# Ends of a two-layer attention and adjacency kernel: first loads by columns, biases of three pairs by accumulating transfers, the bias product on column tiles, a new order

## The chip, the cores and the metric

The kernel runs on one core of a Trainium2 chip. A core has a matrix engine (TensorE, PE in the profile, with its weight loads shown as PEld), a vector engine (VectorE, DVE), a scalar engine (ScalarE, ACT), a general engine (GpSimd, POOL) and an engine that mainly issues transfers (SyncE, SP). Each runs its own instructions in order and waits on semaphores for the others. Transfers between the device's memory (DRAM) and the core's memory (SBUF) are issued by SP, ACT or POOL into queues and carried out by 16 DMA engines. Matrix products go into PSUM, which here is used as eight banks of 128 x 512 f32.

The metric is the device time of one execution in microseconds (us), the median over several runs. The profile is of one execution, which has its own time.

## The reference

Two layers on x of 64 x 256 x 512 (f32), with an adjacency matrix adj of 256 x 256 zeros and ones, 8 heads of 64:

```python
q = (x @ Wq + bq).reshape(b, n, H, HD)          # k, v alike
scores = jnp.einsum('bqhd,bkhd->bhqk', q, k) / jnp.sqrt(jnp.float32(HD))
scores = scores + (1.0 - adj)[None, None, :, :] * -1000000000.0
attn = jax.nn.softmax(scores, axis=-1)
out = jnp.einsum('bhqk,bkhd->bqhd', attn, v).reshape(b, n, d)
x = _layernorm(x + (out @ Wo + bo))             # layer 0
y = jnp.einsum('nm,bmd->bnd', adj, x)
x = _layernorm(x + (y @ W1 + b1))               # layer 1
```

The layer norm has no weights: it subtracts the mean over the 512 features and divides by the root of the variance plus 1e-5.

## The kernel before

**Tiling.** The 64 batches are taken as 32 pairs, p = 0 to 31. A pair has 512 rows, so a product of a pair with a 512 x 512 matrix is four *blocks*, `block(name, p, j)`, each of one bank (`product`, L311 to L337). Names are q, k, v (projections), o (times Wo) and l (times W1). q and k are made transposed, features on partitions; `j` counts feature tiles there and row tiles elsewhere. Heads come in two halves of four (g = 0, 1).

**Precision.** An f32 product is made of three products in the faster type fp32r. Each operand is split into a high part, a low part and a scaled difference (`x_high` and `x_rest` for x, `set_high` and `rest` for the others, `split_high`, `split_rest`, `split_scale` for weights), and a block is 3 x 4 matmuls of 128x512, in the order low, high, diff (`operands`). The high part is a copy on ACT, low and diff are two instructions on DVE, the scale of a weight's low part is again on ACT. Only the first half of pair 0's q and k are plain f32 products of unsplit weights (4 matmuls, each in two halves in the trace).

**Weights.** There is no room for all split weights. A ring of six 1 MB tiles `wr` holds two stages of three parts; `STAGES` (L100) lists them: qk1, v, qk0, then for each pair v, qk1, o, qk0 of the next, l of the last. The first time, a stage is split from raw weights in the ring (`ring_high`, `ring_rest`, `ring_scale`: L122, L127/L128, L131, four steps each) and kept in DRAM (`keep`, POOL). From then on `load_w` (L114, POOL) loads the three parts when `end_stage` has freed a stage. `steps_of` cuts the twelve steps of a stage into four lists, which `start`, `first` and `second` put between blocks.

**Attention.** `scores(p, g)` makes eight banks of logits in matmuls of 64 rows (L414) and the exponentials on ACT (L427); `masked` (L433) multiplies by the adjacency on DVE, two per batch, and `summed` (L441) adds the two key halves. `values(p, g)` multiplies the sums with ones (L370) and the exponentials with v (L380), both on 32-column tiles of the array, copies the banks out on ACT (zc L372, vc L384) and divides on DVE (L387 to L399). Between the two batches of values an argument `between` puts other work.

**Residuals and norms.** `load_r` brings a pair's x as residual R (1 MB, SP). `biased` (L450) adds bo or b1 to one batch of R, 128x1024 on DVE; a block of o or l is added to R while it is evicted (L324, DVE), with the row sums. Then `mean` (DVE), `squared` (ACT), `inverse` (DVE, then a power on POOL, L476), `less` (DVE) and `normed` (L487, ACT), which for l also issues the output. `hl_high` (ACT) and `hl_low` (DVE) split the result, and `adj_x` (L514) multiplies it by the adjacency.

**Start.** SP loads the four row tiles of pair 0's x, bq, bk, Wv, adj, pair 1's x in 128-byte runs (`load_x`, 4 transfers for each of 4 tiles), Wo, bv, bo, b1; ACT's queue loads halves of Wq and Wk (256 columns each). `x_first` (L237) transposes pair 0's x on TensorE against an identity made on POOL, 16 transposes, and copies each 128x128 out alternately on DVE and ACT. `square_adj` checks adj for numbers that aren't finite. `bv_wo` (L226) folds bv into bo, since bv times Wo is the same for all rows: bv is widened to 128 columns, four f32 matmuls make the product in all 128 rows, and DVE adds it to bo.

**Order.** Pairs are pipelined by hand: `first(w)` and `second(w)`, for w = 1 to 30, hold the second half of pair w - 1's attention, pair w's projections, o and l of pair w - 1 and the first q and k of pair w + 1. `start` comes before, `ending` behind. On PE, DVE and ACT instructions run in the order in which these functions write them (L640 to L649); POOL and SP are ordered by a scheduler. A check (`n_good`) at the end decides whether a general version must run instead; with these inputs it doesn't.

Of the kernel before, what the change touches and what calls it, by code (L numbers as in the profile page):

```python
# [8 lines left out]
F32 = mybir.dt.float32  # L9
F32R = mybir.dt.float32r  # L10
I32 = mybir.dt.int32
AF = mybir.ActivationFunctionType
# [23 lines left out]
def fast(tc, x, adj, wq, bq, wk, bk, wv, bv, wo, bo, w1, b1, out):  # L36
# [33 lines left out]
    RAW, SCRATCH, W, UNCUT = {}, {}, {}, {}  # L70
# [17 lines left out]
    def by_partition(b, name):  # L88
        t = cpool.tile([P, DC], F32, name=name)
        nc.sync.dma_start(t, b.rearrange("(c p) -> p c", p=P))  # L90
        return t
# [75 lines left out]
    rows0 = []  # L167
    for i in range(4):
        t = four.tile([P, D], F32, name="low")
        nc.sync.dma_start(t, xc[0, i // 2, i % 2])  # L170
        rows0.append(t)
    for which, w in (("q", wq), ("k", wk)):
        RAW[which] = two.tile([P, DC, D], F32, name="r")
        nc.scalar.dma_start(RAW[which][:, :, 0:HF], w.rearrange("(c p) e -> p c e", p=P)[:, :, 0:HF])
# [3 lines left out]
    bq_s, bk_s = by_partition(bq, "bq"), by_partition(bk, "bk")  # L178
# [3 lines left out]
    for which, w in (("q", wq), ("k", wk)):  # L182
        nc.scalar.dma_start(RAW[which][:, :, HF:], w.rearrange("(c p) e -> p c e", p=P)[:, :, HF:])
    adj_s = two.tile([P, NC, N], F32, name="vc")
    nc.sync.dma_start(adj_s, adj.rearrange("(c p) m -> p c m", p=P))
    for i in range(4):
        load_x(1, i)
    for k in range(DC):
        if k % 2 == 0:
            raw_o = two.tile([P, 2, D], F32, name="hl")  # L190
        RAW["o", k] = raw_o[:, k % 2]
        nc.sync.dma_start(RAW["o", k], wo[k // 2 * HF:(k // 2 + 1) * HF].rearrange("(h a i) e -> a h i e", h=4, a=2)[k % 2])
    bv_s = cpool.tile([P, DC], F32, name="bv")
    for d in range(DC):
        nc.sync.dma_start(bv_s[:, d:d + 1], bv.rearrange("(g h a i u) -> g a h i u", h=4, a=2, i=32, u=1)[d // 2, d % 2])
# [8 lines left out]
    power = cpool.tile([P, 2], F32, name="power")  # L204
    nc.gpsimd.memset(power, -0.5)
    adjT = cpool.tile([P, NC, N], F32R, name="adjT")
# [10 lines left out]
    def square_adj():  # L217

        square = two.tile([P, NC, N], F32, name="vc")
        nc.vector.tensor_tensor(square, adj_s, adj_s, op=OP.mult)  # L220
        nc.vector.tensor_tensor(square, square, adj_s, op=OP.not_equal)
        nc.vector.memset(acc, 0.0)
        nc.vector.tensor_reduce(acc[:, 0, 0:1], square, AX.XY, OP.max)
        nc.vector.tensor_scalar(acc, acc, RANGE * RANGE, None, op0=OP.mult)

    def bv_wo():  # L226

        wide = one.tile([P, DC, P], F32, name="z")
        nc.vector.tensor_copy(wide, bv_s[:, :, None].to_broadcast([P, DC, P]))
        pm = banks.tile([P, D], F32, name="ps")  # L230
        for d in range(DC):
            nc.tensor.matmul(pm, wide[:, d, :], RAW["o", d], start=d == 0, stop=d == DC - 1)
        nc.vector.tensor_tensor(bo_s, bo_s, pm, op=OP.add)
# [3 lines left out]
    def x_first(i):  # L237
        if i == 0:
            for d in range(DC):
                if d % 2 == 0:  # L240
                    t = one.tile([P, 2, D], F32, name=f"e{2 + d // 2}")
                XF[0, d] = t[:, d % 2]
# [3 lines left out]
        for d in range(DC):  # L246
            to = XF[0, d][:, i * P:(i + 1) * P]
            if d % 2:
                nc.scalar.activation(to, pt[:, d], AF.Copy)
            else:  # L250
                nc.vector.tensor_copy(to, pt[:, d])
# [41 lines left out]
    def operands(name, p, j, k):  # L293
# [15 lines left out]
        return [pairs[i] for i in (1, 0, 2)]  # L309

    def product(name, p, j):  # L311
        pm = banks.tile([P, D], F32, name="ps")
        pairs = [operands(name, p, j, k) for k in range(DC)]
        n = len(pairs[0])
        for i in range(n):
            for k in range(DC):
                nc.tensor.matmul(pm, *pairs[k][i], start=i == 0 and k == 0, stop=i == n - 1 and k == DC - 1)  # L317
# [130 lines left out]
    def biased(p, b, bias):  # L448
        if 0 <= p < NP:
            nc.vector.tensor_tensor(R[p][b], R[p][b], bias[:, None, :].to_broadcast([P, NC, D]), op=OP.add)  # L450
# [7 lines left out]
    def mean(p, name, b, cs=slice(0, 2)):  # L458
        if 0 <= p < NP:
            if cs.start == 0:  # L460
                ln = small.tile([P, 4, 2], F32, name="ln")
# [21 lines left out]
    def normed(p, name, j):  # L483
        if 0 <= p < NP:
            b, c = divmod(j, 2)
            t, r = LN[p, name, b], R[p][b][:, c]
            nc.scalar.activation(r, r, AF.Identity, scale=t[2][:, c:c + 1], bias=t[3][:, c:c + 1])  # L487
# [46 lines left out]
    def first(w, more=([], [], [], [])):  # L534

        q, n = w - 1, w + 1
        values(q, 1, ([(x_t, n, 0), (x_t, n, 1), (squared, q - 1, "l", 2)], [(squared, q - 1, "l", 3)]))
        scores(w, 0)
        do((inverse, q - 1, "l", 1), masks(w, 0, 0),
# [15 lines left out]
    def second(w, more=([], [], [], [])):  # L555
        q, n = w - 1, w + 1
        values(w, 0, ([(squared, q, "o", 2), (hl_low, q, 0, 0), (hl_low, q, 0, 1)], [(squared, q, "o", 3)]))
        scores(w, 1)
        masks1 = masks(w, 1, 1)
        do((inverse, q, "o", 1), (with_b1, q, 0), masks(w, 1, 0), more[0],  # L560
           (block, "q", n, 0), (less, q, "o", 1), (normed, q, "o", 2), (normed, q, "o", 3), masks1[:1],
           (adj_x, q, 0, 0), (hl_high, q, 1, 0), (hl_low, q, 1, 0), masks1[1:2], more[1],
           (block, "k", n, 0), (adj_x, q, 0, 1), (hl_high, q, 1, 1), (hl_low, q, 1, 1),
           (qk_high, "q", n, 0), (qk_rest, "q", n, 0), (qk_high, "k", n, 0), (qk_rest, "k", n, 0), more[2],
           (block, "q", n, 1), (adj_x, q, 1, 0), (k_low, n, 0), (qk_high, "q", n, 1), more[3], masks1[2:],
           (block, "k", n, 1), (stage_end, n), (adj_x, q, 1, 1), (qk_high, "k", n, 1), (qk_rest, "q", n, 1),
           (block, "l", q, 0), (qk_rest, "k", n, 1), (k_low, n, 1), (block, "l", q, 1), (with_b1, q, 1),
# [9 lines left out]
    def start():  # L577
        do(*((x_first, i) for i in range(4)), *((x_high, 0, i) for i in range(4)))
        qk1, v, qk0 = (steps_of(*stage) for stage in STAGES[:3])
        do((block, "q", 0, 0), (x_rest, 0, 0), (x_rest, 0, 1), qk1[0], (block, "k", 0, 0), (x_rest, 0, 2), (x_rest, 0, 3), qk1[1],  # L580
           (block, "q", 0, 1), qk1[2], v[0], (block, "k", 0, 1), (square_adj,), (adj_t,), qk1[3])
        scores(0, 0)
        do(v[1], masks(0, 0, 0), (block, "q", 0, 2), v[2], (qk_high, "q", 0, 2), (qk_rest, "q", 0, 2), (x_t, 1, 0), (x_t, 1, 1), v[3],
           (block, "k", 0, 2), (x_high, 1, 0), (x_high, 1, 1), (qk_high, "k", 0, 2), (qk_rest, "k", 0, 2), masks(0, 0, 1),
           (block, "q", 0, 3), (k_low, 0, 2), (qk_high, "q", 0, 3), (qk_rest, "q", 0, 3), (x_rest, 1, 0), (x_t, 1, 2),
           (block, "k", 0, 3), (stage_end, 0), (qk_high, "k", 0, 3), (qk_rest, "k", 0, 3), (x_rest, 1, 1), (x_t, 1, 3), qk0[0],
           (block, "v", 0, 0), (k_low, 0, 3), (x_high, 1, 2), (x_rest, 1, 2), (block, "v", 0, 1), qk0[1],
           (block, "v", 0, 2), (x_high, 1, 3), (x_rest, 1, 3), qk0[2], (block, "v", 0, 3), qk0[3], (stage_end, 0), (load_r, 0), (load_l,))
        values(0, 0)
        scores(0, 1)  # L590
        qk0 = [(f, name, 1, j) for j in range(2) for name in "qk" for f in (qk_high, qk_rest)]
        do((bv_wo,), (block, "q", 1, 0), masks(0, 1, 0), qk0[:2], (block, "k", 1, 0), qk0[2:4], masks(0, 1, 1),
           (block, "q", 1, 1), (k_low, 1, 0), qk0[4:6], (o_high, 0, 0, 0), (o_high, 0, 1, 0), (o_rest, 0, 0, 0),
           (block, "k", 1, 1), qk0[6:], (stage_end, 0), (k_low, 1, 1), (o_rest, 0, 1, 0))

    def ending():
# [37 lines left out]
           (inverse, p, "l", 0), (normed, q, "l", 3),  # L634
# [203 lines left out]
```

## Time and profile before

| what | value |
|---|---|
| time, three runs | 2412.70, 2413.47, 2413.59 us; median 2413.47 |
| the profiled execution's own time | 2412.73 us |
| its span (first to last recorded work) | 2411.0 us |
| DVE's commonest: masked, 128x1024 | 299.7 us in 252, mean 1221 ns |
| squares of the norms on ACT, 128x512 | 184.0 us in 256, mean 719 ns |
| normed on ACT, 128x512 | 194.9 us in 256 (some records hold two), mean of a record 809 ns |
| power on POOL | 152.6 us in 129, mean 1183 ns |
| loads of split weights, 1 MB each | median from issue to landing: 6.8 (v), 7.6 (qk), 8.2 (o), 8.3 (l) us |
| keeps of split weights, 1 MB each | median 9.6 us |
| moved by the DMA engines | 603.45 MB, mean 250 GB/s |

A timeline row is written "start, duration, engine, line, operation, output <- inputs, shape, count", and in brackets the idle time of the engine before it and what ended it. A line number is that of the kernel before. A product's record of 512 f32r columns is about 0.39 long, but matmuls overlap in the pipeline, and a new one starts about every 0.23. The 40 slices of the span show TensorE at 90% or more in all but the first (80 to 90%) and the last (70 to 80%).

### The profile page before, as it was taken

How to read it: one execution, taken by the hardware profiler on the slowest of the kernel's cores; microseconds unless marked ns; L12 is line 12 of the kernel's file. 1: busy time of each engine (PE TensorE's matmuls, PEld its weight loads, DVE VectorE, ACT ScalarE, POOL GpSimd, SP SyncE). 2: the span in 40 equal slices, each digit the busy share in tenths (PEclk: the TensorE clock that was granted, in tenths of full speed). 3: DMA queues.
4: the chain of work that ended last, by engine and by line, in shares of the span. 5: the costliest groups of instructions: out<-in, count | busy, mean ns of one | idle time of the engine just before them, and what ended most of it. 6: DMA issues, size and time to landing. Idle time of an engine off the chain costs nothing.

```text
span 2411.0 us, 42905 instructions
## 1 busy us (share of the span) xinstructions
PE 2382.0 (99%) x16894; PEld 1908.6 (79%) x16894; DVE 2003.9 (83%) x3320; ACT 1504.1 (62%) x2796; POOL 449.5 (19%) x736
## 2 busy tenths in 40 slices
PE   8999999999999999999999999999999999999997
PEld 5778878888778878788887788787888877888876
DVE  7898888888888988888888889888888888898876
ACT  5666665666666666656656566566566565665655
POOL 0111121121121211211212111112122121112111
PEclk9999999999999999999999999999999999999999
DMA  7777787777887777977778877779768788777661
GB/s 251 273 230 266 257 282 260 233 246 257 262 290 243 229 266 253 292 256 229 254 258 262 280 243 237 258 255 299 253 224 261 258 262 274 241 236 261 241 240 37
DMA packets 370719, 603.45 MB, mean 250 GB/s; under 512 B 272848, under 2 KB 275152, under 8 KB 310224
## 3 DMA queue, kind: packets, MB, share of 16 engines
q0 software_dynamic: 67824, 493.91, 55.5%
q1 hardware_dynamic: 300576, 104.64, 20.0%
q8 instruction: 135, 2.21, 0.4%
q10 hardware_dynamic: 2112, 2.10, 0.2%
q14 instruction: 72, 0.59, 0.1%
HBM read 551.29 MB, written 49.28 MB: 249 GB/s over the span
## 4 chain that ended last, share of the span: by engine, by line
PE 91%; DVE 3%; ACT 1%; DMA 1%; issue 0%; POOL 0%; POOLq 0%; DVEq 0%; ACTq 0%; SPq 0%
PE ps L317 68%; PE ps L380 8%; PE ps L414 8%; PE ps L514 5%; PE ps L370 2%; DMA r<-in_x_dram 1%; ACT r L487 0%; ACT waste L470 0%; DVE r L324 0%; DVE wr L128 0%; DVE hl L504 0%; DVE low L268 0%; DVE wr L127 0%; DVE sm L441 0%; DVE r L450 0%
## 5 line engine op out<-in xcount | busy, mean ns | idle before, releaser
L433 DVE TENSOR_TENSOR e<-e,adjT 128x1024 f32<-128x1024 f32 x252 | 299.7, 1221 | 0.2 <-ACT e L427 0.2
L317 PE MATMUL ps<-wr,sl 128*128 128x512 f32 x1008 | 271.6, 391 | 4.6 <-ACT wr L131 3.9
L317 PE MATMUL ps<-low,wr 128*128 128x512 f32 x992 | 271.4, 395 | 0.0
L317 PE MATMUL ps<-wr,sh 128*128 128x512 f32 x1008 | 270.6, 390 | 0.0
L317 PE MATMUL ps<-wr,sd 128*128 128x512 f32 x1008 | 269.7, 389 | 0.0
L317 PE MATMUL ps<-high,wr 128*128 128x512 f32 x992 | 266.5, 390 | 0.0
L317 PE MATMUL ps<-diff,wr 128*128 128x512 f32 x992 | 265.0, 389 | 0.0
L427 ACT ACTIVATE e<-ps 128x512 f32<-128x512 f32 x504 | 253.0, 627 | 8.1 <-PE ps L414 8.1
L470 ACT ACTIVATE waste<-r,ln 128x512 bf16<-128x512 f32 x256 | 184.0, 719 | 108.0 <-DVE ln L463 101.0
L380 PE MATMUL ps<-e,v 128*32 128x256 f32 x4032 | 229.3, 379 | 1.2 <-ACT v L328 1.2
L487 ACT ACTIVATE r<-r,ln 128x512 f32<-128x512 f32 x256 | 194.9, 809 | 53.9 <-DMA x<-in_x_dram 28.5
L476 POOL TENSOR_TENSOR ln<-ln,power 128x2 f32<-128x2 f32 x129 | 152.6, 1183 | 400.8 <-DVE ln L475 342.2
L317 PEld LDWEIGHTS ps<-wr,sh 128*128 128x128 f32 x1008 | 189.8, 188 | 40.1
L317 PEld LDWEIGHTS ps<-wr,sl 128*128 128x128 f32 x1008 | 186.9, 188 | 43.7 <-ACT wr L131 4.7
L317 PEld LDWEIGHTS ps<-wr,sd 128*128 128x128 f32 x1008 | 189.6, 188 | 39.6
L317 PEld LDWEIGHTS ps<-high,wr 128*128 128x128 f32 x992 | 186.1, 188 | 41.2
L317 PEld LDWEIGHTS ps<-diff,wr 128*128 128x128 f32 x992 | 186.2, 188 | 39.1
L337 ACT ACTIVATE uncut<-ps,bq 128x512 f32<-128x512 f32 x126 | 87.1, 692 | 199.7 <-PE ps L317 142.9
L414 PEld LDWEIGHTS ps<-qT,kT 64*128 64x128 f32 x3056 | 188.1, 187 | 27.8 <-PE ps L380 12.3
L349 DVE SCALAR_TENSOR_TENSOR qT<-qT,uncut 128x512 fp32r<-128x512 f32 x126 | 86.7, 688 | 147.0 <-ACT qT L342 147.0
L317 PEld LDWEIGHTS ps<-low,wr 128*128 128x128 f32 x992 | 177.8, 188 | 35.1 <-issue 0.5
L114 POOL DMA_DIRECT2D wr<-qk x183 | 98.5, 539 | 564.4 <-PE ps L317 564.3
(131 smaller groups left out, 4354.3 us busy)
## 6 DMA issues: line engine op xcount, KB each, us to landing
wr<-qk POOLq DMA_DIRECT2D x183, 1024.0 KB, 7.6
wr<-v POOLq DMA_DIRECT2D x93, 1024.0 KB, 6.8
wr<-o POOLq DMA_DIRECT2D x90, 1024.0 KB, 8.2
wr<-l POOLq DMA_DIRECT2D x90, 1024.0 KB, 8.3
r<-in_x_dram SPq DMA_DIRECT2D x32, 1024.0 KB
out_dram<-r SPq DMA_DIRECT2D x62, 512.0 KB
x<-in_x_dram SPq DMA_DIRECT2D x488, 64.0 KB
qk<-wr POOLq DMA_DIRECT2D x6, 1024.0 KB, 9.6
```

The source lines that it names most:

```text
L114: nc.gpsimd.dma_start(W[stage][i], SCRATCH[name, i])
L317: nc.tensor.matmul(pm, *pairs[k][i], start=i == 0 and k == 0, stop=i == n - 1 and k == DC - 1)
L337: nc.scalar.activation(to, pm, AF.Identity, bias=bias[:, j:j + 1], scale=scale)
L349: nc.vector.scalar_tensor_tensor(low, high.bitcast(F32), -RHO, UNCUT.pop((name, p, j)), op0=OP.mult, op1=OP.add)
L380: nc.tensor.matmul(at[h * 32:(h + 1) * 32, a, :], V[p, b][:, kc, col:col + 32], E[p, g, b, kc][0][h % 2][:, h // 2, :], start=kc == 0, sto ...
L414: nc.tensor.matmul(sc[s][:, a, :], K[p, g][r, a, i, keys], Q[p, g][r, a, i, b * N:(b + 1) * N], start=i == digits[0], stop=i == digits[-1])
L427: nc.scalar.activation(e[s], sc[s], AF.Exp, scale=(RHO if (p, g) != (0, 0) else 1.0) * qscale)
L433: nc.vector.tensor_tensor(e, e, mask[:, kc:kc + 1, :].to_broadcast([P, e.shape[1], N]), op=OP.mult)
L470: nc.scalar.activation(waste, R[p][b][:, c], AF.Square, bias=t[0][:, c:c + 1], accum_out=t[1][:, c:c + 1])
L476: nc.gpsimd.tensor_tensor(t[2], t[1], power[:, cs], op=OP.pow)
L487: nc.scalar.activation(r, r, AF.Identity, scale=t[2][:, c:c + 1], bias=t[3][:, c:c + 1])
L514: nc.tensor.matmul(pm[:, j, :], t[:, i, mc, j * P:(j + 1) * P], adjT[:, mc, :], start=mc == 0 and i == 0, stop=mc == NC - 1 and i == 1)
```

## The change

Five things change; the products, their precision and the middle pairs' order stay.

- *First loads.* ACT's queue loads only columns 0 to 127 of Wq. SP loads the four row tiles of x, then columns 128 wide of Wk and Wq, bq and bk, the second halves of both, adj, Wv, half of pair 1's x, Wo, the other half. bv is loaded from POOL's queue. The three small biases share a tile. `x_first` copies 256 columns at a time, even row tiles on DVE, odd ones on ACT.
- *adj.* `test_adj`, one fused instruction with a memset and a scale, takes the place of `square_adj` and stands later; pair 1's first two x transposes (DVE) stand ahead of adj's.
- *bv times Wo.* Four f32 matmuls put four partial products on four 32-column tiles of one bank, ACT copies them out, and a later matmul with a matrix that has ones in rows 0, 32, 64, 96 adds the four and spreads them over all rows (`with_bv`).
- *Biases.* For pairs 0 and 30 both biases, and for pair 31 bo, are added to R by accumulating transfers from POOL's queue (ten of 512 KB); the others stay on DVE.
- *Order.* In `start` the qk0 stage's rests and scales move behind values(0,0) and scores(0,1); q(1,0) and k(1,0) begin with their high products (`begun`), and there and in the last pair's o and l the order is high, low, diff. In `second(1)` the l stage's steps come earlier (the first highs inside values(1,0)) and the masks of half (1,1) later; in `first(2)` x's transposes and the squares follow the scores. `ending` has its last lines reordered; its last `normed` runs on DVE, or half on ACT and half on DVE. The `ln` tiles have four buffers instead of two.

```diff
+    def load_columns(queue, which, a, b):
+        w = wq if which == "q" else wk
+        queue.dma_start(RAW[which][:, :, a:b], w.rearrange("(c p) e -> p c e", p=P)[:, :, a:b])
+
+    load_columns(nc.scalar, "q", 0, P)
     for i in range(4):
         t = four.tile([P, D], F32, name="low")
         nc.sync.dma_start(t, xc[0, i // 2, i % 2])
         rows0.append(t)
-    for which, w in (("q", wq), ("k", wk)):
-        RAW[which] = two.tile([P, DC, D], F32, name="r")
-        nc.scalar.dma_start(RAW[which][:, :, 0:HF], w.rearrange("(c p) e -> p c e", p=P)[:, :, 0:HF])
+    for which, c in ("k", 0), ("q", P), ("k", P):
+        load_columns(nc.sync, which, c, c + P)
...
     def bv_wo():
-        wide = one.tile([P, DC, P], F32, name="z")
-        nc.vector.tensor_copy(wide, bv_s[:, :, None].to_broadcast([P, DC, P]))
         pm = banks.tile([P, D], F32, name="ps")
         for d in range(DC):
-            nc.tensor.matmul(pm, wide[:, d, :], RAW["o", d], start=d == 0, stop=d == DC - 1)
+            nc.tensor.matmul(pm[d * 32:(d + 1) * 32], bv_s[:, d:d + 1].to_broadcast([P, 32]), RAW["o", d], start=True, stop=True)
+        parts = one.tile([P, D], F32, name="z")
+        nc.scalar.activation(parts, pm, AF.Copy)
+        RAW["bv"] = parts
+
+    def with_bv():
+        pm = banks.tile([P, D], F32, name="ps")
+        nc.tensor.matmul(pm, first_of_32.to_broadcast([P, P]), RAW["bv"], start=True, stop=True)
         nc.vector.tensor_tensor(bo_s, bo_s, pm, op=OP.add)
...
-        for d in range(DC):
-            to = XF[0, d][:, i * P:(i + 1) * P]
-            if d % 2:
-                nc.scalar.activation(to, pt[:, d], AF.Copy)
+        for h in range(2):
+            to, of = XF[0, "both", h][:, :, i * P:(i + 1) * P], pt[:, 2 * h:2 * h + 2]
+            if i % 2:
+                nc.scalar.activation(to, of, AF.Copy)
             else:
-                nc.vector.tensor_copy(to, pt[:, d])
+                nc.vector.tensor_copy(to, of)
...
-        return [pairs[i] for i in (1, 0, 2)]
+        soon = p == 1 and name in "qk" and j == 0 or p == NP - 1 and name in "ol"
+        return [pairs[i] for i in ((0, 1, 2) if soon else (1, 0, 2))]
...
+    def begun(name, p, j):
+        BEGUN[name, p, j] = banks.tile([P, D], F32, name="ps")
+        parts_of(BEGUN[name, p, j], name, p, j, (0, 1))
...
     def biased(p, b, bias):
         if 0 <= p < NP:
-            nc.vector.tensor_tensor(R[p][b], R[p][b], bias[:, None, :].to_broadcast([P, NC, D]), op=OP.add)
+            wide = bias[:, None, :].to_broadcast([P, NC, D])
+            if p in (0, NP - 2) or (p == NP - 1 and bias is bo_s):
+                nc.gpsimd.dma_start(R[p][b], wide, accum_op=OP.add)
+            else:
+                nc.vector.tensor_tensor(R[p][b], R[p][b], wide, op=OP.add)
...
-    def normed(p, name, j):
+    def normed(p, name, j, cut=D):
...
+            if cut > 0:
+                nc.scalar.activation(r[:, :cut], r[:, :cut], AF.Identity, scale=scale, bias=bias)
+            if cut < D:
+                nc.vector.tensor_scalar(r[:, cut:], r[:, cut:], scale, bias, op0=OP.mult, op1=OP.add)
...
-    def second(w, more=([], [], [], [])):
+    def second(w):
         q, n = w - 1, w + 1
-        values(w, 0, ([(squared, q, "o", 2), (hl_low, q, 0, 0), (hl_low, q, 0, 1)], [(squared, q, "o", 3)]))
+        high, rest, scale = ([(f, "l", 0, k) for k in range(DC if w == 1 else 0)] for f in (ring_high, ring_rest, ring_scale))
+        values(w, 0, ([(squared, q, "o", 2), (hl_low, q, 0, 0), (hl_low, q, 0, 1), *high[:1]], [(squared, q, "o", 3), *high[1:2]]))
         scores(w, 1)
-        masks1 = masks(w, 1, 1)
-        do((inverse, q, "o", 1), (with_b1, q, 0), masks(w, 1, 0), more[0],
-           (block, "q", n, 0), (less, q, "o", 1), (normed, q, "o", 2), (normed, q, "o", 3), masks1[:1],
-           (adj_x, q, 0, 0), (hl_high, q, 1, 0), (hl_low, q, 1, 0), masks1[1:2], more[1],
+        m = masks(w, 1, 0) + masks(w, 1, 1)
+        if w == 1:
+            m = [high[2:] + rest[:2], m[:1] + scale[:1] + rest[2:], m[1:2] + scale[1:], m[2:3], m[3:4], m[4:]]
+        else:
+            m = [m[:3], m[3:4], m[4:5], [], m[5:], []]
+        do((inverse, q, "o", 1), (with_b1, q, 0), m[0],
+           (block, "q", n, 0), (less, q, "o", 1), (normed, q, "o", 2), (normed, q, "o", 3), m[1],
+           (adj_x, q, 0, 0), (hl_high, q, 1, 0), (hl_low, q, 1, 0), m[2],
            (block, "k", n, 0), (adj_x, q, 0, 1), (hl_high, q, 1, 1), (hl_low, q, 1, 1),
-           (qk_high, "q", n, 0), (qk_rest, "q", n, 0), (qk_high, "k", n, 0), (qk_rest, "k", n, 0), more[2],
-           (block, "q", n, 1), (adj_x, q, 1, 0), (k_low, n, 0), (qk_high, "q", n, 1), more[3], masks1[2:],
+           (qk_high, "q", n, 0), (qk_rest, "q", n, 0), (qk_high, "k", n, 0), (qk_rest, "k", n, 0), m[3],
+           (block, "q", n, 1), (adj_x, q, 1, 0), (k_low, n, 0), (qk_high, "q", n, 1), m[4],
            (block, "k", n, 1), (stage_end, n), (adj_x, q, 1, 1), (qk_high, "k", n, 1), (qk_rest, "q", n, 1),
-           (block, "l", q, 0), (qk_rest, "k", n, 1), (k_low, n, 1), (block, "l", q, 1), (with_b1, q, 1),
+           m[5][:1], (block, "l", q, 0), (qk_rest, "k", n, 1), (k_low, n, 1), m[5][1:], (block, "l", q, 1), (with_b1, q, 1),
...
     def start():
...
-           (block, "v", 0, 0), (k_low, 0, 3), (x_high, 1, 2), (x_rest, 1, 2), (block, "v", 0, 1), qk0[1],
-           (block, "v", 0, 2), (x_high, 1, 3), (x_rest, 1, 3), qk0[2], (block, "v", 0, 3), qk0[3], (stage_end, 0), (load_r, 0), (load_l,))
+           (block, "v", 0, 0), (x_high, 1, 2), high[2:], (k_low, 0, 3), (block, "v", 0, 1), (x_rest, 1, 2), (test_adj,),
+           (block, "v", 0, 2), (x_high, 1, 3), (x_rest, 1, 3), (block, "v", 0, 3), (stage_end, 0), (load_r, 0), (load_l,))
         values(0, 0)
         scores(0, 1)
+        do((bv_wo,), rest[:2], scale[:1], rest[2:3], scale[1:2], rest[3:], scale[2:])
...
-        do((bv_wo,), (block, "q", 1, 0), masks(0, 1, 0), qk0[:2], (block, "k", 1, 0), qk0[2:4], masks(0, 1, 1),
+        m = masks(0, 1, 0) + masks(0, 1, 1)
+        do((begun, "q", 1, 0), (begun, "k", 1, 0), (block, "q", 1, 0), m[:4], qk0[:2], (block, "k", 1, 0), m[4:5], qk0[2:4], m[5:],
            (block, "q", 1, 1), (k_low, 1, 0), qk0[4:6], (o_high, 0, 0, 0), (o_high, 0, 1, 0), (o_rest, 0, 0, 0),
-           (block, "k", 1, 1), qk0[6:], (stage_end, 0), (k_low, 1, 1), (o_rest, 0, 1, 0))
+           (with_bv,), (block, "k", 1, 1), qk0[6:], (stage_end, 0), (k_low, 1, 1), (o_rest, 0, 1, 0))
...
-           (inverse, p, "l", 0), (normed, q, "l", 3),
-           (block, "l", p, 2), (mean, p, "l", 1, c0), (less, p, "l", 0), (squared, p, "l", 2), (normed, p, "l", 0), (normed, p, "l", 1),
-           (inverse, p, "l", 1, c0),
-           (block, "l", p, 3), (mean, p, "l", 1, c1), (less, p, "l", 1, c0), (squared, p, "l", 3), (inverse, p, "l", 1, c1),
-           (normed, p, "l", 2), (less, p, "l", 1, c1), (normed, p, "l", 3))
+           (inverse, p, "l", 0),
+           (block, "l", p, 2), (mean, p, "l", 1, c0), (squared, p, "l", 2), (normed, q, "l", 3, 0), (less, p, "l", 0),
+           (block, "l", p, 3), (mean, p, "l", 1, c1), (inverse, p, "l", 1, c0), (squared, p, "l", 3), (normed, p, "l", 0), (normed, p, "l", 1, 0),
+           (less, p, "l", 1, c0), (inverse, p, "l", 1, c1), (normed, p, "l", 2, 0), (less, p, "l", 1, c1), (normed, p, "l", 3, D // 2))
```

## The prediction

> **What bounds the kernel now.** I read the busy times first, then TensorE's list of waits, then its timeline at the start, at the first l product and at the end.
>
> ```profile
> span 2411.0 us, 42905 instructions
> PE 2382.0 (99%) x16894; PEld 1908.6 (79%) x16894; DVE 2003.9 (83%) x3320; ACT 1504.1 (62%) x2796; POOL 449.5 (19%) x736
> PE ps L245 <- DMA low<-in_x_dram: 5.8, 3, 4.1
> PE ps L317 <- ACT wr L131: 3.9, 2, 3.1
> PE ps L317 <- DVE low L268: 1.9, 2, 1.7
> PE ps L232 <- ACT e L427: 1.7, 1, 1.7
> PE ps L380 <- ACT v L328: 1.2, 1, 1.2
> PE ps L414 <- ACT zc L372: 0.7, 1, 0.7
> PE ps L370 <- DVE sm L441: 0.4, 1, 0.4
> ```
>
> TensorE is busy for 2382.0 of 2411.0. The 29.0 idle are the listed waits (columns: total, times, longest), a few small ones and the tail; none lies between about 152 and 2340 us. So a steady pair costs what TensorE costs, the change leaves that alone, and every term is idle time or a slow clock at an end.
>
> ```profile
> 7.96 2.04 PE L245 MATMUL ps<-z,low 128*128 128x128 f32 x8 [0.78 <-DMA low<-in_x_dram]
> 65.11 3.67 PE L232 MATMUL ps<-hl,z 128*128 128x512 f32 x8 [1.68 <-ACT e L427]
> 68.22 1.49 PE L317 MATMUL ps<-low,wr 128*128 128x512 f32 x4
> 147.40 0.50 PE L317 MATMUL ps<-wr,sl 128*128 128x512 f32 x1 [3.10 <-ACT wr L131]
> 152.30 1.09 PE L317 MATMUL ps<-wr,sl 128*128 128x512 f32 x4
> 143.68:152.30 8.62, 4.69 (x14) 3.23 (x13) 8.45 (x13) 4.88 (x9) 1.61 (x3) 0.80 0.85 315
> 2376.38 1.17 PE L317 MATMUL ps<-wr,low 128*128 128x512 f32 x4 [1.72 <-DVE low L268]
> 2399.94 0.22 PE L656 MATMUL ps<-table,ones 128*32 128x1 f32 x2
> 2404.51 0.81 ACT L487 ACTIVATE r<-r,ln 128x512 f32<-128x512 f32 x1 [0.40 <-DVE ln L481]
> ```
>
> A timeline row begins with start and duration; the bracket is the idle time before. The long row is a window: length, busy time of PE, PEld, DVE, ACT and POOL with counts, then granted TensorE clock, DMA share, GB/s. DVE is busy 8.45 of its 8.62.
>
> **a) First loads.** Rows of x shared the queues with 512 KB of q and k and landed 1.9 apart (transposes at 4.11, 6.06, 7.96). Now only 256 KB of q lie beside them. In the first 12 us 274 GB/s arrived; at that rate 1 MB of x and 256 KB of q take 4.8, so I put the last row at about 6.4 and let four transposes of 1.1 run back to back from 4.11: 8.5. Each half of a bank is now one copy of 256 columns, between the rows of 128 columns (0.29) and 512 (0.69): 0.42, one after the transposes' end. First product at 9.0 instead of 10.88: 1.9 gained. What can cut it is the clock: matmuls of the first product ran at a pitch of 0.86 until 15.28 and 0.43 after, 4.4 after that product began though 11.2 after the first transpose. If that switch stays at 15.28, the work done earlier runs at half speed and about half of the gain, 0.9, is left; if the rows of x land no earlier, 0; if it switches a step sooner, 2.6. POOL issues one tiny transfer (0.53 to 0.73) ahead of the identity; that hides before 4.11.
>
> The Trainium skill ("TensorE: Matmul & The Clock Gate", section "What's actually happening") says that the array runs at half rate until it has been busy over a free-running window of about 3.4 us. The row agrees in the halving, and a free-running window would leave this term at 0.9 or lift it by a whole window; no row here settles its phase.
>
> **b) Pair 0's attention and the ring.** The waits 1.23 (L380), 0.73 (L414) and 1.68 (L232) are all for ACT, which stood behind ring scales (L131) that wait for rests on DVE. Those rests and scales now follow scores(0,1). ACT then has only its copies and exponentials there, and I leave 0.2 of the 3.64: 3.4 gained, 2.0 if one moved rest or scale makes q(1,0) wait (for this each of q(1,0) and k(1,0) begins with its four high products, 0.9 of cover apiece, against a rest pair of 1.33 and a scale). The `qk0` keeps on POOL move too: issued at about 62 and landed by 72 to 75 (wr loads of the same 1 MB take 6.8 to 13.4). The next load of the ring behind them is needed at about 91; 3 of slack after its own time.
>
> **c) bv times Wo.** The old product ran from 65.11 to 68.22: 3.11 for eight half matmuls of 512 f32 columns. The new four sit on four 32-column tiles. Where heads use such tiles, 16 records of 256 columns take 0.89, so they overlap; four f32 matmuls of two records each at 0.43 then take 0.87, and with_bv one more 0.86. Each change of tile mode costs 0.12 (first group 1.19 against 1.07); two are new: 0.25. So 1.98 for 3.11: 1.1 gained; 1.4 with the modes free; if the four tiles ran one after the other, 4 x 0.86 + 0.86 + 0.25 = 4.3, a loss of 1.2.
>
> The Trainium skill ("TensorEngine Tiling (Array Packing)", section "Key Properties") speaks against this edit: a change of tiling mode drains TensorE. It gives no time; the row has 0.12, and even ten times that would leave a loss of only 1.1.
>
> **d) L370 on L441**: 0.4 gained or nothing.
>
> **e) The first l product.** From 143.68 to 152.30 TensorE did 12 matmuls in 8.62; at the usual 0.227 they take 2.72, so 5.9 are lost: 3.10 + 0.83 waiting for wr of L131, and the rest at a granted clock of 0.80. DVE was full there. Now the l steps stand before and between the masks of half (1,1), and those masks follow adj_x(0,1). DVE also loses b1's add of (0,0) and two of bo (1.14 to 1.18 each). By adding up rows the last scale is ready at about 132, its need at 138 of the shifted time. The masks (1.18 each) come later in exchange: the last sum of half (1,1) I get at 148.6 with need at 149.7. Two split copies now precede the evictions of vc in values(1,0): 0.5 lost. Gain 5.4; 5.9 without that loss, 2.4 if the masks are 3 late.
>
> **f) Ending.** High products come first ("soon"), and b1's two adds (2 x 1.15) leave DVE, so L317's waits 1.72 and 0.20 for L268 go: 1.9; if DVE's chain before hl stays as late, half. Waits of 0.32, 0.87 and 0.35 stay.
>
> **g) Tail.** The last eviction queued behind an inverse; the last normed ended at 2405.32, 5.38 after TensorE. Now: eviction 0.68, mean 0.15, square 0.82, inverse 0.15 and POOL 0.55, less 0.16, half a normed of 0.81 and hand-overs: 3.6. Of the 1.8, four closing writes that bunch may take 0.5 (1.5 at worst): 1.3.
>
> **Accumulating transfers.** No row of before shows one. Ten, 512 KB each, take the place of DVE adds, and I cost them at nothing because of cover: b1 of (0,1) stands between hl_low and the eviction of l(0,2), 13 us; pair 30's b1 has 14.2 (2364.06 to 2378.26) and 16.5. Bounds: half of a plain 1 MB wr load, 3.4, and twice the longest, 26.8. I take 8, nearest the plain loads, since a read of the target is added while the bytes halve. Past 13 each us is TensorE's. On POOL's queue, the bo ones wait for R's load. Behind pair 30's stand the wr loads of qk00(31), delayed 3 to 4 with slack about 5; behind pair 31's wr of l(30), about 2 late with slack 15; behind b1 of (0,0) the sums and l's keeps; and behind b1 of (0,1) v(2)'s loads, issued 137 to 142 for 156: 7 of slack by the median landing of 6.8, none by the longest of 13.4. SP loses bv's four transfers, which held it for 22.9 us, so x and R come earlier.
>
> **Sum** against the profiled execution, 2412.73: -1.9 - 3.4 - 1.1 - 0.4 - 5.4 - 1.9 - 1.3 = -15.4, so 2397.3. The median lies 0.74 above that execution: **2398**. Poorer ends: 0 - 2.0 + 1.2 - 0 - 2.4 - 0.9 - 0.3 = -4.4 (2409). Better ends: -2.6 - 3.6 - 1.4 - 0.4 - 5.9 - 1.9 - 1.8 = -17.6 (2396).
>
> **Rivals.** *A: DVE becomes the bound again.* The masks are as many as before and DVE is busy all through 100 to 150; e, b and f fall to their poorer ends: 3.0 + 1.4 + 1.0 more, 2403. For: 8.45 of 8.62. Against: three adds less and 7 us of early scales. *B: slower, by the accumulating transfers.* If one takes 26.8, l(0,2) waits 13.8 and pair 30's l some 12.6: 26.4 on top of 2398, 2424. It decides from 13 us on, breaks even at about 21. For: R is read and written over, and the same queue is at 0.85 of its share in the window above. Against: 512 KB is half of what lands in 6.8 to 8.3. *C: it doesn't do what it says.* Rows of x land no earlier, the l steps are ready no sooner, and one ACT wait stays: 1.9 + 5.4 + 1.4 lost, 2407; with c at its loss, 2409.
>
> **How the numbers follow.** Forecast 0.65, A 0.20, B 0.09, C 0.06. About 0.2% (4.8 us: 2408.6 to 2418.3) can't be told from no change. Faster takes the forecast, A and half of C: 0.86; same the rest of C and a mild B: 0.06; slower B: 0.08. Range 2394 to 2408: below, the better ends less the 1.54 of waits that I leave in the ending; above, past A to C, leaving out B and part of C.
>
> **What would show it.** a: first L317 at 9.0 and its clock. b and d: no wait of L380, L414, L370 or of the biases' product on ACT or DVE. c: a group on 128*32 lasting 0.87. e: no wait at l(0,0), granted clock about 1 there, and none for sm at values(1,1). f: 1.72 gone. g: under 4 from TensorE's last matmul to the last normed. An accumulating transfer over 13 us, a wait of an eviction on DMA, or a new wait in 90 to 160 makes the prediction wrong.

## The result, and the profile after

The changed kernel takes 2444.45 us (median of 4 runs, 2444.33 to 2444.95) against 2413.53 (the median of four runs of before): a ratio of 1.0129, with a 95% interval of 1.0111 to 1.0146. It is 31 us slower where 15 us faster was forecast. Its profiled execution took 2444.33, with a span of 2442.6.

The page of the kernel after, busy times:

```profile
span 2442.6 us, 42940 instructions
PE 2416.0 (99%) x16896; PEld 1909.4 (78%) x16896; DVE 1997.4 (82%) x3308; ACT 1505.3 (62%) x2790; POOL 461.9 (19%) x755
```

The span grew by 31.6, but TensorE's *busy* time grew by 34.0, for two matmuls more. It doesn't wait longer: idle time went from 29.0 to 26.6. Its list of waits (total, times, longest):

```profile
PE ps L409 <- ACT v L357: 8.3, 1, 8.3
PE ps L259 <- POOL numbers L215: 4.9, 1, 4.9
PE ps L553 <- DVE hl L543: 0.8, 1, 0.8
```

The others are of 0.5 or less. L317 of before is L332 here, L370 is L399, L380 is L409. The waits that were to go are gone (L131, L441, L427, and the 1.72 for L268) but for one: that of values(0,0) for ACT's copies of v, 1.23 at L380 before, is 8.35 at L409 now. Lines of TensorE's timeline, at the start, at the biases' product, in the middle of the run and at the end:

```profile
9.56 14.55 PE L332 MATMUL ps<-e,r 128*128 128x512 f32 x32 [0.47 <-ACT e L263]
60.56 5.55 PE L409 MATMUL ps<-e,v 128*32 128x256 f32 x56 [8.35 <-ACT v L357]
69.11 1.06 PE L239 MATMUL ps<-hl,biases 128*32 128x512 f32 x8
70.10 2.13 PE L332 MATMUL ps<-high,wr 128*128 128x512 f32 x8
...
1050.20 1.10 PE L332 MATMUL ps<-wr,sl 128*128 128x512 f32 x4
1051.13 1.09 PE L332 MATMUL ps<-wr,sh 128*128 128x512 f32 x4
1052.06 1.10 PE L332 MATMUL ps<-wr,sd 128*128 128x512 f32 x4
1052.99 1.09 PE L332 MATMUL ps<-wr,sl 128*128 128x512 f32 x4
...
2431.62 0.22 PE L704 MATMUL ps<-table,ones 128*32 128x1 f32 x2
```

The middle lines matter most. The same block of the kernel before:

```profile
1038.09 1.07 PE L317 MATMUL ps<-wr,sl 128*128 128x512 f32 x4
1038.99 1.07 PE L317 MATMUL ps<-wr,sh 128*128 128x512 f32 x4
1039.90 1.07 PE L317 MATMUL ps<-wr,sd 128*128 128x512 f32 x4
1040.81 1.07 PE L317 MATMUL ps<-wr,sl 128*128 128x512 f32 x4
```

Four matmuls start every 0.907 before (1038.09 to 1040.81, three steps) and every 0.93 after, with no wait between them, at the same granted clock. Which operations this touches is seen in the groups of TensorE between 300 and 2100 us (count | busy, mean ns of one | idle), first of before, then of after:

```profile
L317 PE MATMUL ps<-wr,sd 128*128 128x512 f32 x781 | 208.8, 389 | 0.0
L317 PE MATMUL ps<-diff,wr 128*128 128x512 f32 x768 | 205.2, 389 | 0.0
L380 PE MATMUL ps<-e,v 128*32 128x256 f32 x3136 | 178.2, 379 | 0.0
L514 PE MATMUL ps<-adjT,hl 128*128 128x256 f32 x768 | 106.2, 281 | 0.0
```

```profile
L332 PE MATMUL ps<-wr,sd 128*128 128x512 f32 x767 | 209.8, 395 | 0.0
L332 PE MATMUL ps<-diff,wr 128*128 128x512 f32 x768 | 210.3, 395 | 0.0
L409 PE MATMUL ps<-e,v 128*32 128x256 f32 x3072 | 174.6, 379 | 0.0
L553 PE MATMUL ps<-adjT,hl 128*128 128x256 f32 x768 | 106.1, 281 | 0.0
```

Only the blocks' 512-wide matmuls became longer, all alike; attention and adj_x did not. Nothing in the change's text touches these matmuls of the middle pairs. The span by stretches, from TensorE's timelines, with the forecast's terms and the best kernel found below:

| stretch | before | after | difference | forecast | best |
|---|---|---|---|---|---|
| start to the sums of values(1,1) | 160.58 | 158.33 | -2.25 | -12.2 (a to e) | 148.24 |
| from there to those of values(30,1): 29 pairs | 2140.58 | 2175.77 | +35.19 | 0 | 2140.58 |
| from there to the last matmul | 98.83 | 97.58 | -1.25 | -1.9 (f) | 96.59 |
| from there to the span's end | 10.98 | 10.88 | -0.10 | -1.3 (g) | 11.08 |

The rows where the second stretch begins and ends, of before and then of after:

```profile
160.58 1.07 PE L370 MATMUL ps<-sm,ones 128*32 128x256 f32 x16
2301.16 1.07 PE L370 MATMUL ps<-sm,ones 128*32 128x256 f32 x16
```
```profile
158.33 1.07 PE L399 MATMUL ps<-sm,ones 128*32 128x256 f32 x16
2334.10 1.07 PE L399 MATMUL ps<-sm,ones 128*32 128x256 f32 x16
```

A pair takes 75.03 instead of 73.81, in each of the 29.

### The profile page after: what moved, and what is told of

Its sections match the earlier page's. It is cut to its first block, busy times and chain, and to the rows that moved or that the text cites. A ratio compares the mean times of both kernels' runs of the same rounds, so it can differ in the third digit from the quotient of the medians.

```text
span 2442.6 us, 42940 instructions
## 1 busy us (share of the span) xinstructions
PE 2416.0 (99%) x16896; PEld 1909.4 (78%) x16896; DVE 1997.4 (82%) x3308; ACT 1505.3 (62%) x2790; POOL 461.9 (19%) x755
## 4 chain that ended last, share of the span: by engine, by line
PE 95%; SPq 1%; DVE 1%; DMA 1%; ACT 1%; issue 0%; POOL 0%; POOLq 0%; DVEq 0%; ACTq 0%
PE ps L332 71%; PE ps L409 9%; PE ps L443 8%; PE ps L553 5%; PE ps L399 2%; SPq L80 1%; DMA o<-in_x_dram 0%; SPq L202 0%; DMA vc<-in_adj_dram 0%; ACT waste L503 0%; DMA r<-in_L_gnn_Wq_dram 0%; DVE r L353 0%; SPq L171 0%; DVE hl L543 0%; DVE r L483 0%
## 5 line engine op out<-in xcount | busy, mean ns | idle before, releaser
L366 ACT ACTIVATE uncut<-ps,biases 128x512 f32<-128x512 f32 x252 | 172.9, 686 | 286.0 <-PE ps L332 188.2
L332 PE MATMUL ps<-wr,sl 128*128 128x512 f32 x1008 | 276.0, 395 | 0.5 <-DVE sl L282 0.4
L332 PE MATMUL ps<-wr,sh 128*128 128x512 f32 x1008 | 275.7, 395 | 0.0
L332 PE MATMUL ps<-wr,sd 128*128 128x512 f32 x1008 | 275.5, 395 | 0.0
L332 PE MATMUL ps<-low,wr 128*128 128x512 f32 x992 | 275.1, 399 | 0.0
L332 PE MATMUL ps<-diff,wr 128*128 128x512 f32 x992 | 271.7, 395 | 0.0
L332 PE MATMUL ps<-high,wr 128*128 128x512 f32 x992 | 270.7, 394 | 0.0
L409 PE MATMUL ps<-e,v 128*32 128x256 f32 x4032 | 231.6, 382 | 8.3 <-ACT v L357 8.3
L524 ACT ACTIVATE r<-r,ln 128x512 f32<-128x512 f32 (+1 forms) x253 | 192.2, 808 | 55.7 <-DVE ln L514 31.3
L332 PEld LDWEIGHTS ps<-wr,sd 128*128 128x128 f32 x1008 | 189.5, 188 | 45.2
L332 PEld LDWEIGHTS ps<-wr,sh 128*128 128x128 f32 x1008 | 189.6, 188 | 45.0
L332 PEld LDWEIGHTS ps<-high,wr 128*128 128x128 f32 x992 | 186.3, 188 | 45.4 <-ACT e L456 0.8
L332 PEld LDWEIGHTS ps<-diff,wr 128*128 128x128 f32 x992 | 186.7, 188 | 44.7
L509 POOL TENSOR_TENSOR ln<-ln,numbers 128x2 f32<-128x2 f32 x129 | 148.3, 1150 | 386.5 <-DVE ln L508 379.0
L332 PEld LDWEIGHTS ps<-wr,sl 128*128 128x128 f32 x1008 | 187.0, 188 | 43.9 <-DVE sl L282 1.2
L332 PEld LDWEIGHTS ps<-low,wr 128*128 128x128 f32 x992 | 178.4, 189 | 37.7 <-ACT wr L129 0.6
L409 PEld LDWEIGHTS ps<-e,v 128*32 128x32 f32 x4032 | 131.7, 111 | 96.8 <-ACT v L357 8.8
```

Source lines behind the costliest of these rows:

```text
L366: nc.scalar.activation(to, pm, AF.Identity, bias=bias[:, j:j + 1], scale=scale)
L409: nc.tensor.matmul(at[h * 32:(h + 1) * 32, a, :], V[p, b][:, kc, col:col + 32], E[p, g, b, kc][0][h % 2][:, h // 2, :], start=kc == 0, sto ...
L509: nc.gpsimd.tensor_tensor(t[2], t[1], power[:, cs], op=OP.pow)
L524: nc.scalar.activation(r[:, :cut], r[:, :cut], AF.Identity, scale=scale, bias=bias)
```

## The experiments

**Where tiles lie.** What the change does alter for the middle pairs is where tiles start in SBUF. Per partition, the pool of the split parts (x and set parts) lies ahead of the ring `wr`. By the sizes of the tiles in the kernels' text, 114048 bytes of tiles lie ahead of the first part in before and 114016 in after, and the ring begins 49152 and 49280 bytes behind the first part. So both start at remainder 0 by 128 in before and 96 in after. The constants shrank by 32 bytes, and the `ln` tiles of 32 bytes, two in the pool `small` behind the ring before, are four now in the pool of the parts, ahead of the ring. Two theories: alignment of the starts (A), or something in the new transfers and order (the rival).

`after_aligned`:
```diff
+    wring = pool("wr", 6)
+    four = pool("four", 4)
     cpool = pool("consts", 1)
...
-    four = pool("four", 4)
-    wring = pool("wr", 6)
```


> The kernel after with the pools of the weight ring and of the split parts made ahead of the others, so that these tiles start at multiples of 128 bytes again (after: remainder 96; before: 0). No instruction changes. Theory A (the 512-wide products run slower because their operands lost their alignment): the period of a pair goes from 75.03 back to 73.81, and 29 such periods give 35.4, with some 3 more in the start and the ending: 2405 to 2409. Rival (the slower products come from the transfers or the order): the period stays 75.03 and the time 2444.

2408.47, ratio 0.9979 (0.9970 to 0.9989), a pair 73.83. With the same instructions in the same order, 36 us are gone. The rival fell: transfers and order don't slow the middle.

`after_wr_first`, the ring alone:
```diff
+    wring = pool("wr", 6)
     cpool = pool("consts", 1)
...
-    wring = pool("wr", 6)
```


> The kernel after with only the weight ring's tiles back at multiples of 128; the split parts stay at remainder 96. Theory A where the moving operand decides: blocks v, o and l, whose moving operand is wr, are back at 0.227 a matmul and q and k stay slow: 12 of 20 blocks, period near 74.3, time near 2423. Theory A where the stationary operand decides: q and k are back, v, o and l stay slow: 8 of 20, period near 74.5, time near 2430. Rival (not alignment): 75.03 and 2444.

2452.14, ratio 1.0162 (1.0145 to 1.0179), a pair 75.27. All blocks were slow, q and k as well as v, o and l, and slower than in after. Neither form of theory A said so.

`before_pad32` and `before_pad64`:
```diff
-    power = cpool.tile([P, 2], F32, name="power")
+    power = cpool.tile([P, 10], F32, name="power")
```
```diff
-                ST[p, name, b] = two.tile([P, 2], F32, name="sums")
+                ST[p, name, b] = small.tile([P, 2], F32, name="sums")
```


> The kernel before with one small constant tile 32 bytes longer, which puts ring and split parts at remainder 32 of 128 and all else 32 bytes on. Theory A: the period goes from 73.81 to about 75.0 and the time from 2413.5 to 2449 to 2452, though no instruction of the change is in it. Rival: 2413.5.

> The kernel before with two small tiles (the row sums) moved behind the ring, which puts ring and split parts at remainder 64 of 128; everything else stays where it was. Theory A with 64 bytes as the unit: 2413.5 and a period of 73.81. Theory A with 128 bytes as the unit: slower by as much as the kernel with remainder 32. Rival: 2413.5.

2413.66 (ratio 1.0001, 0.9991 to 1.0010) and 2414.06 (1.0007, 0.9997 to 1.0016), pairs of 73.81 and 73.84. Theory A fell: parts and ring may both start at remainder 32 or 64. What is left is the *distance* between parts and ring: these two keep the 49152 of before, and the two slow kernels have others (49280 and -163168). That is theory B. In every block of pairs 1 to 31 one operand is a part and the other is in the ring.

`after_ln_behind` and `before_gap128`, each other's reverse:
```diff
     wring = pool("wr", 6)
+    behind = pool("behind", 4)
...
-                ln = four.tile([P, 4, 2], F32, name="ln")
+                ln = behind.tile([P, 4, 2], F32, name="ln")
```
```diff
+    between_ = pool("between", 2)
     wring = pool("wr", 6)
...
-        rz = small.tile([P, n], F32, name="rz")
+        rz = between_.tile([P, n], F32, name="rz")
```


> The kernel after with its four ln tiles (128 bytes) taken out from between the split parts and the weight ring. Ring and parts start at remainder 96 of 128 as in the kernel after, but the distance from the parts to the ring is 49152 bytes again, as in the kernel before; after has 49280. No instruction changes. Theory B (what decides is the distance between a matmul's stationary and moving operand): back to a period of 73.8 and 2405 to 2410. Theory A (remainder 96 of 128 is bad, 0, 32 and 64 are not): 75.03 and 2444.

> The kernel before with a small tile of 128 bytes (rz) moved between the split parts and the weight ring: both still start at multiples of 128, the distance is 49280 as in the kernel after. Theory B: period about 75 and time about 2449. Theory A: 73.81 and 2413.5.

2407.25, ratio 0.9976 (0.9966 to 0.9986), and 2450.49, ratio 1.0156 (1.0139 to 1.0173). Theory B held both ways. The groups of before_gap128, which has not one instruction of the change, beside those of after above:

```profile
L318 PE MATMUL ps<-wr,sd 128*128 128x512 f32 x768 | 209.9, 395 | 0.0
L318 PE MATMUL ps<-diff,wr 128*128 128x512 f32 x768 | 210.3, 395 | 0.0
L381 PE MATMUL ps<-e,v 128*32 128x256 f32 x3072 | 174.6, 379 | 0.0
```

They are those of after to the nanosecond of the mean. Then the unit, with tiles of other sizes between parts and ring of the kernel before (64: the row sums; 256: rz and seen; 512: these, `ln`, the sums and `ones`; 1024: waste; 2048: zc), one run each, every edit of the form of before_gap128:

> The kernel before with a small tile of 64 bytes (the row sums) between split parts and ring: distance 49216; the parts are where they were in before_pad64, which was fast, and the ring where it was in before. Theory B in its strict form (any distance that is not a multiple of an operand's row of 2048 bytes): period 74.5 to 75.3, time 2435 to 2455. If only some distances do it: 73.8 and 2414.

> The kernel before with 256 bytes of small tiles (rz, seen) between split parts and ring: distance 49408, a multiple of 256 but not of 512 bytes. If the unit of the distance is 512 (a stationary operand's 128 f32 of a partition) or 1024: slow, a period of 74.5 to 75.3, 2435 to 2455. If it is 256: 73.8 and 2413.

> The same with 512 bytes of small tiles between them: distance 49664. If the unit is 512 or 256: 73.8 and 2413. If it is 1024: slow, 74.5 to 75.3, 2435 to 2455.

> The same with a tile of 1024 bytes (waste) between them: distance 50176, a multiple of 1024 but not of 2048. If a multiple of 512 or 1024 is enough: 73.8 and 2414. If it must be 2048: 74.5 to 75.3 and 2435 to 2455.

> The same with a tile of 2048 bytes (zc): distance 51200, a multiple of 2048. Theory B in both forms: 73.8 and 2414. If it is the sheer presence of a tile between parts and ring, or another tile's place, that decides: about 75 and 2450.

| kernel | first ring tile less first part, bytes | remainder by 256 | a pair | time |
|---|---|---|---|---|
| before | 49152 | 0 | 73.81 | 2413.53 |
| before_pad32 | 49152 | 0 | 73.81 | 2413.66 |
| before_pad64 | 49152 | 0 | 73.84 | 2414.06 |
| after_ln_behind | 49152 | 0 | 73.81 | 2407.25 |
| before_gap64 | 49216 | 64 | 74.53 | 2435.09 |
| before_gap128 | 49280 | 128 | 75.03 | 2450.49 |
| after | 49280 | 128 | 75.03 | 2444.45 |
| before_gap256 | 49408 | 0 | 73.81 | 2412.15 |
| before_gap512 | 49664 | 0 | 73.84 | 2413.76 |
| before_gap1024 | 50176 | 0 | 73.81 | 2413.15 |
| before_gap2048 | 51200 | 0 | 73.81 | 2412.90 |
| after_aligned | -49152 | 0 | 73.83 | 2408.47 |
| after_wr_first | -163168 | 160 | 75.27 | 2452.14 |

The strict form (2048) and the units 512 and 1024 fell. All kernels with a distance that is a multiple of 256 bytes are fast, and the three other distances (64, 128 and 160 over such a multiple) slow; no others were run.

What it looks like shows in the starts of a pair's v product, which follows scores (64-row tiles). Nanoseconds from one start to the next, before (from 1053.86 on) and then after (from 1066.17 on):

```
335 231 236 228 232 231 227 226 227 227 226 227 227 226 227 ...
334 233 232 228 230 232 241 233 231 231 229 230 232 241 232 ...
```

In both the first ones are disturbed. Before, the pace is back at 227 after six; after, the disturbance goes round (230, 232, 241, 233) until matmuls of another kind come. Why the distance should do that inside the engine no run here tells.

**The wait of 8.35.** Three views of the kernel after: ACT's, DVE's and SP's timelines. SP's row is of eight transfers, the third and fourth tile of pair 1's x.

```profile
57.84 0.63 ACT L278 ACTIVATE high<-xT 128x512 fp32r<-128x512 f32 x1 [14.56 <-DVE xT L270]
```
```profile
57.10 0.71 DVE L270 STREAM_TRANSPOSE xT<-o 128x512 f32<-128x512 f32 x1 [11.58 <-DMA o<-in_x_dram]
```
```profile
20.21 5.64 SPq L202 DMA_DIRECT2D hl<-in_L_gnn_Wo_dram  x4
25.89 30.38 SPq L80 DMA_DIRECT2D o<-in_x_dram  x8
```

The chain runs backwards: the eviction of v waits behind `x_high` on ACT, that for DVE's transpose, that for x. The transfers held SP for 30.38; before, they stood ahead of Wo, and the last in the queue were bv's four:

```profile
17.68 4.21 SPq L80 DMA_DIRECT2D o<-in_x_dram  x8
27.63 22.93 SPq L195 DMA_DIRECT2D bv<-in_L_gnn_bv_dram  x4
```

`aligned_x_first` is after_aligned with x ahead of Wo again:
```diff
     for i in range(4):
-        if i == 2:
-            for k in range(DC):
...
         load_x(1, i)
+    for k in range(DC):
...
```


> The kernel after_aligned, with all four tiles of pair 1's x loaded before Wo again. Theory S (the 8.35 us stall at L409 is the third and fourth x tile, which stand behind Wo in SP's queue and wait there while POOL's 1 MB keeps take the engines): the stall goes, less a few tenths, and the time is 2400 to 2401.5. Rival (the stall is ACT's new order in start, not the transfer): 2408. A new wait may come for Wo at the biases' product, which then loads later: up to 8 back.

2403.35, ratio 0.9961 (0.9947 to 0.9975). The wait at L409 is gone, so theory S holds, and the wait that the expectation warned of came in its place:

```profile
63.10 1.89 PE L238 MATMUL ps<-hl,biases 128*32 128x512 f32 x2 [5.95 <-DMA hl<-in_L_gnn_Wo_dram]
```

So whoever stands last in SP's queue from about 26 to 57 us is late: bv before, x in after, Wo in aligned_x_first. In after, SP's queue moved 3576 packets of 128 bytes and 451 of 2048 between 26 and 57, 1.4 MB, while POOL's moved 811 of 8192, 6.6 MB: the keeps of split weights and the first reloads. The Trainium skill ("DMA: Bandwidth & Descriptors", section "SWDGE vs HWDGE vs iDMA") says that a DMA engine serves its queues in turn; turns of unequal size agree with the bytes, though the packets here were not one for one. No run moved POOL's transfers, so their part in the delay is argued, not shown.

**The biases on DVE.** `aligned_dve_bias`, from after_aligned:
```diff
-            if p in (0, NP - 2) or (p == NP - 1 and bias is bo_s):
+            if False:
                 nc.gpsimd.dma_start(R[p][b], wide, accum_op=OP.add)
```


> The kernel after_aligned with all biases added on DVE (ten adds of 128x1024 in place of the ten accumulating transfers). If the transfers bring what was forecast (two adds off DVE in the ending, three near the first l), it is slower than after_aligned by 1 to 4: 2409 to 2412. If DVE has room for the adds: 2408.5. If the transfers cost something: below 2408.

2411.04, ratio 0.9991 (0.9981 to 1.0000), against after_aligned's 0.9979 (0.9970 to 0.9989): the medians are 2.6 apart, but the intervals overlap. The profiles, one of each, show where: the stretch from values(30,1) to the last matmul takes 97.64 instead of 96.56, and from values(1,1) to values(2,1), right behind l of pair 0, 75.11 instead of 73.83. There scores wait for DVE's evictions of l, which now stand behind an add of b1:

```profile
163.92 0.97 PE L443 MATMUL ps<-qT,kT 64*128 64x256 f32 x11 [0.91 <-DVE r L353]
```

From values(0,1) to values(1,1) it is 75.43 and 75.44. So I read 1.1 for the transfers in the ending, 1.3 behind the first l product and nothing ahead of it, 2.4 in all and about what the medians say.

**The forecast's kernel.** `behind_x_first_bv_late` puts three things right in after: `ln` behind the ring, x ahead of Wo, and the product of the biases later:
```diff
-        do((bv_wo,), rest[:2], scale[:1], rest[2:3], scale[1:2], rest[3:], scale[2:])
+        do(rest[:2], scale[:1], rest[2:3], scale[1:2], rest[3:], scale[2:])
...
-           (block, "q", 1, 1), (k_low, 1, 0), qk0[4:6], (o_high, 0, 0, 0), (o_high, 0, 1, 0), (o_rest, 0, 0, 0),
-           (with_bv,), (block, "k", 1, 1), qk0[6:], (stage_end, 0), (k_low, 1, 1), (o_rest, 0, 1, 0))
+           (block, "q", 1, 1), (bv_wo,), (k_low, 1, 0), qk0[4:6], (o_high, 0, 0, 0), (o_high, 0, 1, 0), (o_rest, 0, 0, 0),
+           (block, "k", 1, 1), (with_bv,), qk0[6:], (stage_end, 0), (k_low, 1, 1), (o_rest, 0, 1, 0))
```


> The kernel after with three things put right: ln behind the ring (distance 49152), all of pair 1's x loaded ahead of Wo, and the four small matmuls of the biases' product moved behind block q(1,1), with_bv behind block k(1,1), so that Wo may land some 8 us later. Against aligned_x_first, the wait of 5.9 for Wo should go, less a few tenths for two more changes of tile mode: 2397.5, range 2396.5 to 2399. If it comes back as another wait in pair 1, 2400 to 2403.

2397.51, ratio 0.9933 (0.9919 to 0.9947): 16 us faster than before, 47 faster than after. Its waits:

```profile
PE ps L259 <- DMA low<-in_x_dram: 5.9, 3, 3.8
PE ps L553 <- DVE hl L543: 1.0, 2, 0.9
```

The others are of 0.5 or less.

## Why the prediction was wrong, point by point

**The step that failed** is the first: "a steady pair costs what TensorE costs, the change leaves that alone". TensorE does bound the kernel, but its cost per matmul isn't a constant of the kernel: four buffers of `ln` in a pool ahead of the ring instead of two behind it, a place that the prediction names nowhere, moved the ring by 128 bytes against the parts, and 29 pairs cost 1.21 more each, 35.2 in all. The sum had no term for it and none of the rivals was near it; B had the right side for a cause that didn't happen.

The forecast's own terms add up in the best kernel, 2397.51 for 2398, but partly by luck: a brought 0.15 of 1.9 in its profile and g nothing of 1.3, b and c 5.1 of 4.5, d and e 7.1 of 5.8.

**a)** First product at 9.56, not 9.0: 1.3 of the 1.9. The rest hung on the clock, as the working had it: full speed, a pitch of 0.43, came at 11.07 in after, at 15.28 before and at 15.56 in the best kernel. So the matmuls behind the first four products began at 23.95 in after, 26.87 before and 26.72 in the best: 2.9 gained, or 0.15. Kernels with the same first loads had their first product between 8.54 and 10.61, so its start alone is worth 0.3 to 2.3 from one execution to the next.

**b)** Its three waits went, but another wait took their place on the same path: ACT's copies of v now stood behind x. The working had "SP loses bv's four transfers ... so x and R come earlier" and took the queue's length for the landing; half of x had moved behind Wo into POOL's busy time. Cost: 8.35 less the 1.23 that was there before, and a slow clock behind it. After the wait 56 matmuls took 5.49 to the next group at a granted clock of 0.57; in the best kernel 64 take 3.56 (53.78 to 57.34). That is 2.4 more. The window in after, then the row of the best kernel:

```profile
60.56:66.05 5.49, 5.49 (x58) 2.45 (x58) 5.28 (x12) 2.64 (x5) 0.58 (x3) 0.57 1.12 327
```
```profile
53.78 3.64 PE L409 MATMUL ps<-e,v 128*32 128x256 f32 x64
```

**c)** The four-tile product took 0.99 to the next matmul (69.11 to 70.10; 1.0 forecast with its change of mode), so the tiles do overlap. The poorer end was added up short: 4 x 0.86 + 0.86 + 0.25 is 4.55, a loss of 1.4 and not 1.2.

**d, e)** No wait for L441, none at the first l product. TensorE had no gap in this window of the kernel after (length, busy times, clock, DMA share, GB/s):

```profile
146.00:158.00 12.00, 12.00 (x57) 9.91 (x56) 11.45 (x18) 3.70 (x7) 1.45 (x3) 1.00 1.07 379
```

The clock is 1.00 where it was 0.80. DVE at 11.45 of 12.00 did not become the bound (rival A), and the l steps were ready in time (against C). In the best kernel a to e together bring 12.3 of the forecast's 12.2.

**f)** 2.2 in the best kernel for 1.9; 1.25 in after, where the blocks are slow.

**g)** 0 for 1.3. The last normed ended 4.0 after TensorE's last matmul instead of 5.4 (2435.02 + 0.60 against 2431.62), but the span's end stayed 10.9 behind that matmul: the closing writes and SP's waits for them took the other 1.3, near the 1.5 that the working had as its worst.

**Accumulating transfers (B).** Landing in after, median us of six and of four:

```profile
r<-bo POOLq DMA_DIRECT2D x6, 512.0 KB, 9.9
r<-b POOLq DMA_DIRECT2D x4, 512.0 KB, 5.3
```

Single ones took 5.0 to 15.8, those of b1 at most 9.6, within the 13 to 16 of cover; the 8 taken was about right, and no wait for them is in the list. Two of bo's, 15.8 and 14.6, passed the 13 that the prediction named as a sign; no eviction waited for them. B did not happen. (The chances of faster don't add up as stated: 0.65, 0.20 and half of 0.06 are 0.88, not 0.86.)

## What to carry to other kernels

After any edit that adds, drops or resizes a tile, compare the pace of the steady loop's matmuls before looking for waits: a busy time that grows with no new work points at where operands lie. Keep operands that meet in one 512-wide fp32r matmul at a distance of a multiple of 256 bytes, as all fast kernels here had it, by giving small tiles a pool behind the large ones. And when a transfer is moved back in a queue, ask what other queues move by then, not only how long the queue ahead of it is.

## What the runs showed of the hardware

A 128x512 fp32r matmul starts every 227 ns, steady, where its operands lie a multiple of 256 bytes apart; in after it falls into a pattern of a few matmuls with a mean of 232 to 234, by that distance alone. A pair took 73.81 to 73.84 in the fast kernels, and 74.53, 75.03 and 75.27 at remainders 64, 128 and 160. The 256-wide ones kept their pace (281 ns a record in adj_x, both kernels), but by the kernels' text none of these edits changed the distance of their operands, so nothing here says whether they mind it. The first matmuls behind another kind are disturbed even in the fast kernels: behind scores 335, 231, 236, 228, 232, 231 ns, and behind adj_x, whose matmuls use the same whole array but are 256 wide, 239, 227, 231, 236, 228, 232, 231. A wait of TensorE of 8.35 was followed by 5.49 at a granted clock of 0.57. Issuing an accumulating transfer held POOL for 1.2 to 1.8 us, where a plain 1 MB load held it for 0.54.
